# Attention blocks through DRAM: which side of the round trip is cut into four transfers

## The chip, the cores and the metric

The kernel runs on one core of a Trainium2 chip. The metric is the device time of one execution in microseconds (us). A core has five engines with a queue each: TensorE (PE in the profile, its weight loads PEld), VectorE (DVE), ScalarE (ACT), GpSimd (POOL) and SyncE (SP). SP computes nothing here; its queue issues nearly all DMA transfers, in program order, so a transfer that waits holds up every transfer behind it.

## The reference

A gated cross-attention block followed by a mixture of experts, all in float32. For each of 32 batch entries, 112 latent rows of 256 features attend to 375 context rows and to themselves, 487 keys in all, with 16 heads of 64 features. The result, times tanh of a gate, is added to `x`; then each token goes through its best two of eight experts.

```python
x = layer_norm(x, ln_m_g, ln_m_b)                  # context, 375 rows
lat = layer_norm(latents, ln_l_g, ln_l_b)          # 112 rows
q = lat @ Wq
k, v = jnp.split(jnp.concatenate([x, lat], axis=1) @ Wkv, 2, axis=-1)
dots = jnp.einsum('bhid,bhjd->bhij', q, k) * scale
attn = jax.nn.softmax(dots, axis=-1)
out = jnp.einsum('bhij,bhjd->bhid', attn, v)       # then @ Wout
...
x = x + jnp.tanh(g_xattn[0]) * attention(x, ctx)
x = x + jnp.tanh(g_ffn[0]) * experts(layernorm(x)) # top 2 of 8, gelu
```

## The kernel before

The program is one long list of steps without hardware loops. The attention stage fills about the first 1490 us, the expert stage the rest; at the seam they overlap.

Attention goes by *units* `n` from 0 to 127. A unit is one batch entry with two pairs of heads, so four heads, and two units (two batch entries, the same heads) make a *period*; there are 64. Scores are computed with queries on the partitions: the 112 queries lie as four groups of 28, each padded to 32, and the 487 keys, padded to 512, on the free axis. The exponentials of a unit fill a buffer `ex` (`exs[n % 3]`) of 128 partitions by 2048 float32, that is 8 KB a partition and 1 MB in all. The second matmul, probabilities times values, needs keys on the partitions instead. The turn is made in two steps:

- `turn_blocks` (L574): VectorE transposes every 32x32 block of `ex` in place, inside its group of 32 partitions. Partition `a*32+j` then holds, for query group `a`, key `j` of each block of 32 keys; on the free axis lies the block number `k` (0 to 3, the slowest), then heads, chunks of 128 keys and the query.
- a round trip through DRAM that exchanges `a` and `k`: `send_blocks` (L580) writes the unit to a DRAM buffer `turned[n % 4]`, and `take_blocks` (L587) reads it back as `exT`, where partition `k*32+j` is a key within a chunk of 128 and the free axis holds `a` first. `exT` has two buffers, one for each unit of a period.

The sends and the returns are issued on SP's queue, among the loads of inputs (`xin` L274, `cin` L278, `x` L626) and the transfers with which expert weights are read, added up by POOL and written back as `ws` (`piece_in` L1375 and L1379, `piece_out` L1415 and L1419).

The order of work is written out by hand. A period begins with `attend` of the period before (L600, 64 matmuls that read both `exT` buffers); then come the scores (L536) and exponentials (L555) of the next period's two units, and ten slots (two groups of five) with the steps of the table `PLAN`: `norm` (L569), `turn_blocks`, the query, key and value projections, and the sends `s0` and `s1`. The returns of a period are issued after its second slot:

```python
if h == 1 and not late and n < LAST - 2:
    for s in (n, n + 1):
        take_blocks(s)
if h == 1:
    do(after)                     # loads and pieces
if h == 1 and n == LAST - 2:      # in the last period: after them
    for s in (n, n + 1):
        take_blocks(s)
```

So a period's two units are sent in the period before, come back early in the period itself, and are read by `attend` at the beginning of the next one. A return can't start before `attend` has finished with the old contents of its buffer, nor before the unit's sends have landed. Waits are set by the framework from the tiles that an instruction reads and writes. Transfers from SP and ACT take eight completion semaphores in turn; a transfer also waits until the one that used its semaphore before, eight transfers earlier, has landed.

Of the kernel before, what the change touches and what calls it, by code (L numbers as in the profile page):

```python
# [23 lines left out]
def kernel(  # L24
# [20 lines left out]
    nc = tc.nc  # L45
# [38 lines left out]
    KTB, EXB, ETB = 4, 3, 2  # L84
# [18 lines left out]
    QB, QW, Q = 4, 32, S // 4  # L103
# [17 lines left out]
    turned = [dram.tile([QB, QW, QB, 2 * NCK * 2 * QW], F32, name=f"turned_{n}") for n in range(4)]  # L121
# [70 lines left out]
    if True:  # L192
# [309 lines left out]
        pss, nmx, sm, exT = {}, {}, {}, {}  # L502
# [3 lines left out]
        exs = [const.tile([P, QB, 2, NCK, 2, QW], F32, name=f"ex_{n}") for n in range(EXB)]  # L506
# [68 lines left out]

        def send_blocks(n, eng=nc.sync):


            for a in range(QB):
                eng.dma_start(  # L580
                    turned[n % 4][:, :, a, :].rearrange("k j n -> j k n"),
                    exs[n % EXB][a * QW : (a + 1) * QW].rearrange("j k q c h r -> j k (q c h r)"),
                )

        def take_blocks(n):
            exT[n] = soft.tile([P, QB, 2, NCK, 2, QW], F32, tag="exT", name=f"exT_{n}", bufs=ETB)
            nc.sync.dma_start(  # L587
                exT[n].rearrange("p a q c h r -> p (a q c h r)"),
                turned[n % 4].rearrange("k j a n -> (k j) (a n)"),
            )  # L590

        def attend(j):

# [930 lines left out]
        norm(1, 0)  # L1524
        turn_blocks(0, 1)
        send_blocks(0)
        units[0, 1][6]()
        norm(1, 1)
        turn_blocks(1, 0)
        weight_sums(0, 2)  # L1530
        units[0, 1][1]()
        turn_blocks(1, 1)
        send_blocks(1)
        units[1, 0] = seven(1, 0, 0)
        for kv, k in PROLOGUE:
# [17 lines left out]
        for n in range(LAST):  # L1553
# [17 lines left out]
            def step(what, period=period, beside=beside, qn=qn):  # L1571
                s, p = int(what[1]), int(what[-1])
                if what[0] == "q":
                    for j in qn:
                        q_unit(j // NG, j % NG + NG * s)
                elif what[0] in "kv":
                    at = beside[what[0]]
                    if at[1] < (UNITS, UNITS // 2)[at[0]]:
                        if at not in units:
                            units[at] = seven(*at)  # L1580
                        units[at][p - 1]()
                elif period + 1 < UNITS:
                    s += 2 * (period + 1)
                    if what[0] == "n":
                        norm(s, p)
                    elif what[0] == "t":
                        turn_blocks(s, p)
                    else:
                        send_blocks(s)
# [24 lines left out]
            k = n - 44  # L1614
# [89 lines left out]
            for h in range(5):  # L1704
                for what in PLAN[5 * late + h].split():
                    step(what)
                do(pe[h])
# [4 lines that stand above are left out]
                    do(after)  # L1712
                if h == 1 and n == LAST - 2:
                    for s in (n, n + 1):
                        take_blocks(s)
                if h == 4:
                    break
                then_ = soon_[:]
                del soon_[:]
                do(then_)  # L1720
                for part in dve[h]:
                    part()

                if outgoing and (h % 2 == 0 or n > LAST - NG):
                    outgoing.pop(0)()
                if extra and not (late and h > 1 and isinstance(extra[0], tuple)):
                    do(extra.pop(0))
# [3 lines left out]
        r, _ = route_parts(g, nc.vector)  # L1731
# [130 lines left out]
```

## Time and profile before

| what | us |
|---|---|
| median of three runs (lowest, highest) | 1905.92 (1905.05, 1910.44) |
| the profiled execution, its own time | 1907.72 |
| its span in the profile | 1905.9 |
| PE busy | 1876.3 |
| DVE busy | 1353.5 |
| ACT busy | 1136.4 |
| POOL busy | 992.5 |

The DMA queue that SP and ACT feed, q1, moved 413.31 MB in 247232 packets, and its packets took 73.6% of the 16 DMA engines' span. The 512 sends are of 256 KB each and the 128 returns of 1024 KB. The median issue of a send takes SP 691 ns and that of a return 412 ns.

An engine's busy time says how much it did, not whether it set the end: that is read from the waits, in which each engine's idle time is put down to what ended it. The `L` numbers are lines of the kernel before. The profile was taken on one execution, so sums made from its rows stand against that execution's own time.

### The profile page before, as it was taken

What the parts mean: (1) busy time and instruction counts of PE and PEld (TensorE: products, weight loads), DVE (VectorE), ACT (ScalarE), POOL (GpSimd) and SP (SyncE); (2) the same over time, 40 slices, a digit from 0 to 9 for tenths busy, and PEclk for the clock granted to TensorE, in tenths of its full rate; (3) what the DMA queues carried; (4) which work ended last, traced back from release to release, by engine and by line L of the source; (5) the groups of instructions that cost most, each with busy time, mean ns of one, the idle gap of its engine ahead of it and who ended that gap; (6) DMA issues with size and microseconds to landing.
All of it is one profiled execution on the core that took longest, in us unless ns stands there. A gap on an engine that the chain in (4) does not pass through costs nothing. (4 is left out here: it accounts for less than half of the span.)

```text
span 1905.9 us, 38258 instructions
## 1 busy us (share of the span) xinstructions
PE 1876.3 (98%) x12560; PEld 1433.5 (75%) x12560; DVE 1353.5 (71%) x2868; ACT 1136.4 (60%) x2718; POOL 992.5 (52%) x1475
## 2 busy tenths in 40 slices
PE   8999999999999999999999999999999999999998
PEld 4667777677777676777676777677677999999887
DVE  6787878787877878787878787878776477844111
ACT  5767666666776666667766666666756334434333
POOL 6433333435445746585556655753334588877212
PEclk9999999999999999999999999999999999999999
DMA  7777766767788888798979898896668786897872
GB/s 202 193 229 209 214 196 198 205 182 205 226 227 265 253 246 251 230 280 250 271 224 284 233 268 242 252 265 195 198 184 256 244 240 180 245 336 232 231 205 46
DMA packets 261049, 433.23 MB, mean 227 GB/s; under 512 B 30728, under 2 KB 149072, under 8 KB 244464
## 3 DMA queue, kind: packets, MB, share of 16 engines
q1 hardware_dynamic: 247232, 413.31, 73.6%
q0 software_dynamic: 11328, 15.33, 4.2%
q10 hardware_dynamic: 2288, 2.12, 0.4%
q8 instruction: 101, 1.65, 0.3%
q14 instruction: 100, 0.82, 0.1%
HBM read 301.37 MB, written 172.28 MB: 249 GB/s over the span
## 5 line engine op out<-in xcount | busy, mean ns | idle before, releaser
L555 ACT ACTIVATE ex<-bank,nmx 128x512 f32<-128x512 f32 x512 | 343.6, 697 | 85.7 <-DVE nmx L546 85.2
L569 ACT ACTIVATE ex<-ex,rc 128x512 f32<-128x512 f32 x512 | 342.7, 721 | 76.1 <-DVE rc L566 75.4
L546 DVE TENSOR_REDUCE nmx<-bank 128x1 f32<-128x487 f32 x512 | 298.6, 655 | 85.9 <-PE bank L536 83.6
L574 DVE STREAM_TRANSPOSE ex<-ex 128x1024 f32<-128x1024 f32 x256 | 314.9, 1230 | 19.5 <-ACT ex L569 15.7
L487 POOL TENSOR_TENSOR vv<-tmpv,vv 128x512 f32<-128x512 f32 x64 | 82.1, 1282 | 404.1 <-ACT vv L475 403.4
L536 PE MATMUL bank<-kT,qTs 64*128 64x487 f32 x1024 | 236.3, 588 | 3.0 <-DVE kvT L365 1.7
L600 PEld LDWEIGHTS bank<-exT,vv 128*64 128x64 f32 (+1 forms) x4096 | 198.9, 137 | 30.9 <-issue 22.6
L600 PE MATMUL bank<-exT,vv 128*64 128x112 f32 (+1 forms) x4096 | 213.0, 261 | 2.3 <-DMA exT<-turned 1.6
L617 ACT COPY outT<-bank 128x256 f32<-128x256 f32 (+3 forms) x160 | 40.0, 314 | 263.9 <-PE bank L600 258.8
L434 PE MATMUL bank<-tT,wkv_s 128*128 128x487 f32 x378 | 186.3, 575 | 0.5 <-ACT ex L555 0.5
L439 PE MATMUL bank<-wkv_s,tT 128*128 128x256 f32 x768 | 186.7, 379 | 0.0
L439 PEld LDWEIGHTS bank<-wkv_s,tT 128*128 128x128 f32 x768 | 144.8, 190 | 43.3 <-issue 21.4
L1164 POOL DMA_INDIRECT out_dram<-y,xs x60 | 93.5, 1558 | 154.0 <-DVE y L1191 77.9
L536 PEld LDWEIGHTS bank<-kT,qTs 64*128 64x128 f32 x1024 | 98.8, 187 | 99.2 <-issue 69.9
L1405 POOL TENSOR_TENSOR piece<-piece 128x128 f32<-128x128 f32 x256 | 116.9, 457 | 89.7 <-DMA piece<-in_L_ffn_w_dram 78.3
L439 PE MATMUL bank<-wkv,kvT 128*128 128x256 f32 x512 | 132.0, 380 | 0.8 <-ACT ex L555 0.6
L439 PEld LDWEIGHTS bank<-wkv,kvT 128*128 128x128 f32 x512 | 94.6, 190 | 50.5 <-issue 33.9
L484 DVE TENSOR_TENSOR kT<-bank,kT 128x487 f32<-128x487 f32 x189 | 120.8, 640 | 14.0 <-POOL kT L487 7.5
L434 PE MATMUL bank<-kvT,wkv 128*128 128x487 f32 x252 | 130.1, 598 | 0.0
L484 DVE TENSOR_TENSOR vv<-bank,vv 128x512 f32<-128x512 f32 x192 | 128.2, 668 | 1.8 <-POOL vv L487 0.2
L1219 ACT ACTIVATE h<-h,b 128x256 f32<-128x256 f32 x160 | 66.1, 495 | 91.9 <-DVE h L1230 53.2
L373 PEld LDWEIGHTS bank<-kvT,wq_sb 128*128 128x128 f32 x512 | 96.2, 188 | 28.9 <-issue 17.0
(296 smaller groups left out, 3718.2 us busy)
## 6 DMA issues: line engine op xcount, KB each, us to landing
turned<-ex SPq DMA_DIRECT2D x512, 256.0 KB
exT<-turned SPq DMA_DIRECT2D x128, 1024.0 KB
w<-in_L_ffn_w_dram SPq DMA_DIRECT2D x132, 256.0 KB
w_s<-ws SPq DMA_DIRECT2D x80, 256.0 KB
w_t<-ws SPq DMA_DIRECT2D x80, 256.0 KB
w_b2x<-in_L_ffn_w_dram SPq DMA_DIRECT2D x38, 512.0 KB
ws<-piece SPq DMA_DIRECT2D x64, 256.0 KB
cin<-in_ctx_dram SPq DMA_DIRECT2D x32, 336.0 KB
```

The lines of the kernel that those rows point to most:

```text
L373: nc.tensor.matmul(ps, lhsT=wq_sb[:, k, i * P : (i + 1) * P], rhs=kvT[g][:, k, :, SC:NK], start=(k == 0), stop=(k == KD - 1),)
L434: nc.tensor.matmul(ps, lhsT=w[:, 0, i * P : (i + 1) * P], rhs=x[:, :NK], start=True, stop=True)
L439: nc.tensor.matmul(ps[:, c, :], lhsT=x[:, (2 * h + c) * P : (2 * h + c + 1) * P], rhs=w[:, 1, i * P : (i + 2) * P], start=True, stop=True,)
L484: nc.vector.tensor_tensor(v[o], ps, v[r], ALU.add)
L536: nc.tensor.matmul(ps[:, :NK], lhsT=qT[b // 2, i][r, b % 2].rearrange("p a i -> p (a i)"), rhs=kT[b, i][r, :], start=True, stop=True,)
L546: nc.vector.tensor_reduce(nmx[b, i][:, j : j + 1], pss[b, i][j][:, :NK], AX.X, ALU.max, negate=True)
L555: nc.scalar.activation(exs[n % EXB][:, :, p, :, j, :], ps[j].rearrange("p (c k r) -> p k c r", c=NCK, r=QW), AF.Exp, bias=nmx[b, i][:, j : ...
L569: nc.scalar.mul(t, t, rc[:, j : j + 1])
L574: nc.vector.transpose(t, t)
L600: nc.tensor.matmul(ps[y * DH : (y + 1) * DH, r, x * S : (x + 1) * S].rearrange("p (a i) -> p a i", a=QB), lhsT=vv[j // 2, c // 2][:m, c % ...
L1164: add = nc.gpsimd.indirect_dma_start(out=outf, out_offset=bass.IndirectOffsetOnAxis(ap=xs[t][:, b, D + 1 : D + 2].bitcast(I32), axis=0), i ...
L1405: nc.gpsimd.tensor_tensor(o, l, r, op) for o, l, r, op in ops
```

## The change

The same 1 MB of each unit goes out and comes back with the same bytes in the same places of DRAM. Before, the exchange of `a` and `k` is made on the way out: four sends, one for each query group, each from 32 partitions in runs of 2 KB, scattered into `turned`; the return is one transfer into 128 partitions with runs of 8 KB. After, the send is one transfer from 128 partitions in 8 KB runs, and the exchange is made on the way back: four returns, one for each `k`, each into 32 partitions with runs of 2 KB. The places of the sends and returns in the program's order are the same. The number of transfers per unit stays five.

```diff
         def send_blocks(n, eng=nc.sync):
 
-
-            for a in range(QB):
-                eng.dma_start(
-                    turned[n % 4][:, :, a, :].rearrange("k j n -> j k n"),
-                    exs[n % EXB][a * QW : (a + 1) * QW].rearrange("j k q c h r -> j k (q c h r)"),
-                )
+            eng.dma_start(
+                turned[n % 4].rearrange("a j k n -> (a j) (k n)"),
+                exs[n % EXB].rearrange("p k q c h r -> p (k q c h r)"),
+            )
 
         def take_blocks(n):
             exT[n] = soft.tile([P, QB, 2, NCK, 2, QW], F32, tag="exT", name=f"exT_{n}", bufs=ETB)
-            nc.sync.dma_start(
-                exT[n].rearrange("p a q c h r -> p (a q c h r)"),
-                turned[n % 4].rearrange("k j a n -> (k j) (a n)"),
-            )
+            for k in range(QB):
+                nc.sync.dma_start(
+                    exT[n][k * QW : (k + 1) * QW].rearrange("p a q c h r -> p a (q c h r)"),
+                    turned[n % 4][:, :, k, :].rearrange("a j n -> j a n"),
+                )
```

## The prediction

> **What bounds the kernel now.** I read part 1 of the page first, then the list of who waits for whom on TensorE (PE) and on SP's queue, then SP's timeline through one dense stretch, the DMA view of stretches that hold one kind of transfer, and last the packet records.
>
> ```profile
> PE 1876.3 (98%) x12560; PEld 1433.5 (75%) x12560; DVE 1353.5 (71%) x2868; ACT 1136.4 (60%) x2718; POOL 992.5 (52%) x1475
> ```
>
> And from the waits of PE (who is waited for: us in total, times, longest):
>
> ```profile
> PE bank L600 <- DMA exT<-turned: 1.6, 1, 1.6
> ```
>
> PE sets the time. It is idle for 1905.9 - 1876.3 = 29.6 us, so no transfer change can win more than that; the idle time sits in the start-up, the expert stage and the drain. The wait above is all that PE waits for returned blocks today: one, in the last attend. So the change acts only by making PE late, or by removing that 1.6 us.
>
> ```profile
> 606.00:1260.00 654.00, 653.93 (x4179) 465.53 (x4179) 515.39 (x1072) 439.13 (x1042) 391.02 (x651) 1.00 0.87 254
> 629.00:650.00 21.00, 21.00 (x142) 14.54 (x142) 16.55 (x31) 14.17 (x34) 18.29 (x23) 1.00 0.96 296
> ```
>
> These are stretches of the span: length, PE, PEld, DVE, ACT, POOL busy, clock, DMA share, GB/s. PE has no gap, but the DMA engines are 87% busy over 654 us and 96% in some periods. The cover is thin there.
>
> ```profile
> 627.61 1.45 SPq L1419 DMA_DIRECT2D ws<-piece  x1
> 629.61 4.23 SPq L580 DMA_DIRECT2D turned<-ex  x4
> 633.94 1.18 SPq L274 DMA_DIRECT2D xin<-in_x_dram  x1
> 635.16 1.59 SPq L278 DMA_DIRECT2D cin<-in_ctx_dram  x2
> 636.79 0.90 SPq L1375 DMA_DIRECT2D piece<-in_L_ffn_w_dram  x2
> 637.89 0.38 SPq L1419 DMA_DIRECT2D ws<-piece  x1
> 638.37 0.92 SPq L587 DMA_DIRECT2D exT<-turned  x2
> ```
>
> This is SP's queue between a pair's second send (629.61) and its returns (638.37). Only the returns have 8 KB packets on this queue (16384 = 128 x 128), so the last of each 128 tells when it ends; PE resumed 0.74 us after it in the one place where it waited (1489.20 to 1489.94). For this pair that is 648.29 + 0.74 = 649.03, and the attend that reads it begins at 649.61: 0.58 us of slack. I did this for all 63 pairs before the last. The twelve smallest slacks are 0.58, 0.65, 0.76, 1.39, 1.56, 1.67, 1.73, 1.91, 2.08, 2.12, 2.26, 2.30 us; 21 lie under 4.5; the median is near 6.7. All the small ones but one lie between 578 and 1282 us.
>
> **Price of the two shapes.** Three windows of the DMA view: only sends (258.5 to 262 us), only 2 KB loads into all 128 partitions (1478 to 1482), almost only returns (1482.5 to 1487).
>
> ```profile
> DMA packets 418, 0.77 MB, mean 221 GB/s; under 512 B 41, under 2 KB 41, under 8 KB 418
> ...
> DMA packets 742, 1.36 MB, mean 341 GB/s; under 512 B 77, under 2 KB 77, under 8 KB 742
> ...
> DMA packets 262, 1.86 MB, mean 414 GB/s; under 512 B 23, under 2 KB 23, under 8 KB 40
> ```
>
> The engines are 98 to 100% busy in all three. So 1.05 MB costs 1.05 / 0.221 = 4.7 us as four quarters of 32 partitions, 3.1 us as 2 KB runs over all partitions, 2.5 us as 8 KB runs.
>
> **Sends, removed and added.** 512 sends become 128. Data: the one 8 KB send to DRAM has no row; the return is its mirror, so 2.5 us, 2.2 saved on each of two sends a period. It can't cost more than the 4.7 us of today's send, which moves the same bytes in more pieces; that end would hand back nothing. Issue on SP: 4.23 us for four in the lines above becomes one of about 0.41 (median of a whole-block return), 3.8 saved. Little of that reaches the returns: xin (L274) waits there for PE for 1.1 us whatever the sends do, so the returns can be issued perhaps 0.7 us earlier.
>
> **Returns, removed and added.** 128 become 512. Data: their shape is the send's mirror (32 partitions, 2 KB runs), so I take 4.7 us each: +2.2 each, +4.4 a pair. The low end is the 341 GB/s row, 3.1 us, +1.2 a pair. The high end is the stretch of a send in which its first two quarters are alone, about 190 GB/s in the DMA view of 258.9 to 260.9 us: 5.5 us, +6 a pair. I choose 4.7 because the partition count, not the run length, separates the first two rows.
> [...]
> Issue on SP: eight issues at the send's median 0.69 us are 5.5 us instead of 0.95. Behind them stand two piece loads (0.9) and the next first send, issued 7.6 us after the returns here (645.93). 5.5 + 0.9 = 6.4 fits; at the crowded 4.23 / 4 = 1.06 each it is 9.4 and that send is 1.8 us late, whose waiters are its own returns some 12 us later. Left at nothing; the high end carries it.
>
> **Semaphores.** Transfers use eight completion semaphores in turn, so a transfer waits for the one eight before it. Eight returns take them all; the piece load behind waits for the first quarter (1.2 us of data, issued 5 us before) and passes. PE's first matmul on each buffer waits for four transfers instead of one: 384 more waits. A wait record on PE's queue is 51 ns, so between 0 and 384 x 51 ns = 20 us; I take 0, because PE's queue runs ahead (one such record at 146.53 us precedes its matmul at 150.05) and the existing ones leave PE no gap. StreamTranspose (L574) and exp (L555) wait for one send instead of four: about 0.1 us earlier a block, at nothing.
>
> **The sum.** In a dense period a pair's returns end 4.4 us later for their own data, 2.2 earlier because the second send leaves the ring sooner; what the first send saves is idle ring before the second, which is held by DVE, and the 0.7 us of earlier issue I set against ring gaps. Shift: +2.2 us. PE loses what exceeds each slack: (2.2 - 0.58) + (2.2 - 0.65) + (2.2 - 0.76) + 0.81 + 0.64 + 0.53 + 0.47 + 0.29 + 0.12 + 0.08 = 7.6 us over ten periods. The cover is the slack itself: at a shift of 1 the loss is 1.0 us, at 3 it is 17.5, at 4.5 it is 45. The low end (1.2 - 2.2, below zero) loses nothing. The last pair has no cover:
>
> ```profile
> 1487.36 0.99 PE L600 MATMUL bank<-exT,vv 128*64 128x112 f32 x16 [0.72 <-DVE h L1237]
> 1489.94 3.94 PE L600 MATMUL bank<-exT,vv 128*64 128x112 f32 x48 [1.59 <-DMA exT<-turned]
> ```
>
> PE already waits there for the second return. Its data comes up to 4.4 us later, no send is left to hand anything back; the first return's delay meets PE's own 0.72 us wait. Between 1.2 and 4.4, I take 3.0. Sum: 7.6 + 3.0 = 10.6 us. The profiled execution took 1907.72 us for a span of 1905.9, and its like would take 1918.3; that is 1.8 above the median of 1905.92, so the median becomes 1916.5.
>
> **Rivals.**
> 1. *The cover holds* (not slower). Place: the returns between 578 and 1282 us. If the ring gives back what it takes (a 2 KB return at 341 GB/s, or the sends' 2.2 us each both counting), the shift is 1 us or less, and only the tail costs: 1.0 + 1.2 to 3 = 2 to 4 us, 1908 to 1910. It decides from a shift below about 1.5 us (2.6 us lost). For it: PE has shown no wait at all so far. Against: three slacks under 0.8.
> 2. *The DMA engines become the bound.* At 5.5 us a return the pair costs 6 us more and the sends give 4.4 back, so 1.6 us more work a period. At 96% of 21 us (20.2 us) this makes 21.8: over. Backlog then carries from period to period; with a shift of 4.5 to 6 the losses are 45 to 85 us, less what PE's lateness itself frees, so 20 to 50: 1926 to 1956. For it: the 0.96 row. Against: the mean of 0.87.
> 3. *Faster.* The one wait (1.6 us) and the start-up hold nearly all that transfers could free; more than 3 us has no place to come from.
> 4. *Nothing changes in the transfers* is excluded by the diff: the pieces on both sides are fixed by the patterns.
>
> **How the numbers follow.** Forecast (1911.7 to 1926) 0.45; cover holds 0.27; DMA-bound 0.24; faster 0.04. About 0.3% (5.7 us) is what a measurement of this kernel can tell from no change, so faster 0.04, same 0.27, slower 0.69. The range takes in the cover's case from 1904 and the DMA-bound case up to 1942, leaving out its upper half and the faster case. The forecast's own range is 1911 to 1926.
>
> **What would show it.** Right: a window with only sends near 400 GB/s, one with only returns near 220; PE waits on exT at L600 in some ten periods between 578 and 1282 us, a few us in sum each at most; the last attend's wait 3 to 6 us instead of 1.6. Wrong: returns at 340 GB/s or more; no new L600 wait; or DMA share at 1.0 over hundreds of us with waits growing from period to period; or PE gaps at L600 with the returns long landed, which would be the 384 waits.

## The result, and the profile after

Five runs of the changed kernel took 1920.75 to 1925.73 us, median 1922.93; the kernel before, now with five runs (the three of the table among them), 1905.05 to 1913.14, median 1910.44. The ratio is 1.0073 (95% interval 1.005 to 1.0097): slower by some 14 us. The prediction was a median of 1916.5, that is 10.6 us more than the 1905.92 it was built on, in a range of 1904 to 1942.

The profiled execution took 1920.97 us for a span of 1919.3, against 1907.72 and 1905.9: 13.4 us more of span. In the changed kernel the send is L578, the return L586 and the attend L599. PE's busy time grew by 4 us and its idle time by 9. Part 1 of its page:

```profile
PE 1880.5 (98%) x12560; PEld 1438.5 (75%) x12560; DVE 1352.7 (70%) x2868; ACT 1136.5 (59%) x2718; POOL 992.3 (52%) x1475
```

The waits of PE in the changed kernel (us in total, times, longest). They were one wait of 1.6 us on returned blocks:

```profile
PE bank L599 <- DMA exT<-turned: 6.5, 4, 3.1
PE bank L599 <- issue: 3.6, 1, 3.6
```

The 3.6 us put down to "issue" are the first wait of the last attend. The trace's record of it on PE's queue runs from 1490.50 to 1494.45 us and waits for the semaphores of the first unit's first and fourth quarter; the fourth one's last count came at 1494.41. So this is a wait for a return too. SP's timeline of the changed kernel in the same dense period as shown before:

```profile
628.77 0.33 SPq L578 DMA_DIRECT2D turned<-ex  x1
629.19 0.38 SPq L274 DMA_DIRECT2D xin<-in_x_dram  x1
629.63 2.02 SPq L278 DMA_DIRECT2D cin<-in_ctx_dram  x2
631.75 0.97 SPq L1374 DMA_DIRECT2D piece<-in_L_ffn_w_dram  x2
637.07 0.38 SPq L1418 DMA_DIRECT2D ws<-piece  x1
637.50 4.28 SPq L586 DMA_DIRECT2D exT<-turned  x8
641.83 1.54 SPq L1374 DMA_DIRECT2D piece<-in_L_ffn_w_dram  x2
```

The second send costs SP 0.33 us instead of 4.23, and eight returns 4.28 instead of 0.92. The loads behind the send go out 4 us earlier, but `ws` (L1418) then waits for POOL until 637.07, and the returns gain nothing in this period: they start 0.9 us sooner on the profile's clock, but the second send is 0.8 us earlier there too. The DMA view of two stretches of the changed kernel, the first with sends alone (809 to 811 us), the second with returns alone (245 to 252):

```profile
DMA packets 103, 0.84 MB, mean 422 GB/s; under 512 B 0, under 2 KB 0, under 8 KB 0
...
DMA packets 799, 1.46 MB, mean 209 GB/s; under 512 B 84, under 2 KB 84, under 8 KB 799
```

The two rates have changed sides: before, sends ran at 221 GB/s and returns at 414. What it does to PE, first in a period of the dense stretch, then at the last attend:

```profile
832.80 0.99 PE L599 MATMUL bank<-exT,vv 128*64 128x112 f32 x16
835.68 3.69 PE L599 MATMUL bank<-exT,vv 128*64 128x112 f32 x38 [1.89 <-DMA exT<-turned]
...
1494.61 1.76 PE L599 MATMUL bank<-exT,vv 128*64 128x112 f32 x16 [3.60 <-issue]
1499.46 4.75 PE L599 MATMUL bank<-exT,vv 128*64 128x112 f32 x48 [3.09 <-DMA exT<-turned]
```

PE runs its first 16 matmuls, which read the first unit, and then stops for the second. After these two stops the same matmuls take longer: 48 of them 4.18 and 4.75 us, against 2.53 at 650.64 us, behind a stop of 0.87 us. The windows of the changed kernel show the granted clock there (length, PE, PEld, DVE, ACT, POOL busy, clock, DMA share, GB/s):

```profile
830.00:840.00 10.00, 8.11 (x76) 6.50 (x76) 5.13 (x11) 1.55 (x4) 7.28 (x10) 0.83 1.08 326
1490.00:1505.00 15.00, 8.31 (x76) 7.41 (x75) 1.96 (x4) 3.74 (x10) 1.77 (x5) 0.66 1.07 283
606.00:1260.00 654.00, 650.45 (x4155) 463.87 (x4155) 510.57 (x1062) 435.68 (x1036) 385.87 (x643) 1.00 0.93 251
```

The granted clock falls to half for 3.41 us at 836 us and for 10.24 us from 1495. The kernel before had one such stretch of 3.41 us at its last attend, and one at 66 us, which this execution lacks. Its window over the last attend:

```profile
1485.00:1500.00 15.00, 12.69 (x108) 11.40 (x108) 3.90 (x11) 3.90 (x10) 2.58 (x7) 0.89 0.97 333
```

By the starts of the attends in the two profiles the 13.4 us divide so:

| stretch | us | made of |
|---|---|---|
| to 628 us | -0.8 | start-up +0.9; the half-clock stretch at 66 us is missing, -1.7 |
| 628 to 1428 us | +5.9 | three waits at L599 (0.87, 1.89, 0.69) = 3.45; half clock 3.41 / 2 = 1.7; 0.7 not put down to anything |
| to the start of the last attend | +2.2 | its first wait 3.60 against 0.72; other waits -0.7 |
| from there to the end | +6.1 | its second wait 3.09 against 1.59; half clock 1.9 more; the expert stage +2.7 |

The 1.9 us are read from the lengths: the first 16 matmuls of the last attend take 1.76 us against 0.99, the other 48 take 4.75 against 3.94, and the stretch runs 0.7 us, at half rate, past them. Half of 10.24 - 3.41 would be too much, since PE stands still for 3.09 us of the stretch and a lower clock costs nothing there. The +2.7 can't be put down to the change: what follows the last attend takes 412.1 us before and 415.1 after, but 413.7 to 417.3 us in the eight kernels below.

### The profile page after: what moved, and what is told of

It reads as the page before. It is cut to its first block, busy times and chain, and to the rows that moved or that the text cites. A ratio compares the mean times of both kernels' runs of the same rounds, so it can differ in the third digit from the quotient of the medians.

```text
span 1919.3 us, 38314 instructions
## 1 busy us (share of the span) xinstructions
PE 1880.5 (98%) x12560; PEld 1438.5 (75%) x12560; DVE 1352.7 (70%) x2868; ACT 1136.5 (59%) x2718; POOL 992.3 (52%) x1475
## 3 DMA queue, kind: packets, MB, share of 16 engines
q8 instruction: 102, 1.67, 0.4%
## 5 line engine op out<-in xcount | busy, mean ns | idle before, releaser
L599 PEld LDWEIGHTS bank<-exT,vv 128*64 128x64 f32 (+1 forms) x4096 | 202.0, 139 | 39.3 <-issue 28.8
L599 PE MATMUL bank<-exT,vv 128*64 128x112 f32 (+1 forms) x4096 | 216.8, 264 | 10.1 <-DMA exT<-turned 6.5
```

The lines of the kernel that those rows point to most:

```text
L599: nc.tensor.matmul(ps[y * DH : (y + 1) * DH, r, x * S : (x + 1) * S].rearrange("p (a i) -> p a i", a=QB), lhsT=vv[j // 2, c // 2][:m, c % ...
```

## The experiments

Theory M: a quarter of 32 partitions moves at half the rate (209 GB/s against 414), so returns land later, and PE waits where the slack is short and at the last pair. Theory W: the 384 further waits on PE's queue, or the greater number of transfers, cost the time. Rival R: the 2 KB runs on the return do. Each ratio is to runs of the kernel before on the same chip.

**The last pair in the old shape, all others in the new** (and next, the reverse).

```diff
+            if n >= B * NG - 2:
+                ...  # four sends, one return
+            else:
+                ...  # one send, four returns
```

> The changed kernel, but the last two units (the last period's pair) go out in four sends and come back in one return, as before the change. Theory M (late returns: a return cut into quarters of 32 partitions moves at about 220 GB/s, so a pair lands some 2 us later; PE stalls in the few periods with little slack, and most of all at the last pair): the changed kernel's profile shows 3.60 + 3.09 us of PE waits at the last attend against 0.72 + 1.59 before, and 10.2 us of half clock right behind them against 3.4. So this kernel should win back (6.69 - 2.31) + 6.8 / 2 = 7.8 us of the 13 and stand 4 to 7 us over the kernel before (ratio 1.002 to 1.004), with its last attend waiting 1 to 2.5 us and the waits between 640 and 1110 us still there. Theory W (the 384 further semaphore waits on PE's queue cost the time): 126 of 128 units still have them, so it stays at 1.007.

Measured: ratio 1.0029 (1.0017 to 1.0042). Its PE waits on returned blocks, and a window over its last attend:

```profile
PE bank L612 <- DMA exT<-turned: 3.5, 4, 1.1
...
1486.00:1501.00 15.00, 13.90 (x137) 12.78 (x136) 6.55 (x15) 3.89 (x10) 3.38 (x13) 1.00 1.03 373
```

Three of the four waits are those of the dense stretch (0.91, 1.00 and 0.54 us, at 651, 836 and 1107), the fourth is the last attend's. There is no half clock in that window; the one stretch of it, 3.41 us from 1478.8, lies ahead of it, behind a stop of PE for `xs`, which is no part of the round trip. The expectation's 7.8 us counted half clock also while PE stood still; with 1.9 us for it, 6.3 were to be won back. More than half the loss, 0.44 of 0.73%, went with two units of 128.

> The kernel before, but the last two units go out in one send and come back in four returns. Theory M: the last attend waits 5 to 7 us in all instead of 2.3, and the clock falls for longer behind it: 5 to 9 us over the kernel before (ratio 1.003 to 1.005), and no PE wait on returned blocks anywhere else. Theory W: six waits more in all, nothing measurable: ratio 1.000. If the middle of the attention stage carries the loss instead, also 1.000.

Measured: ratio 1.0023 (1.001 to 1.0035), a little under the range expected. Its PE waits on returned blocks, PE in its last attend, and the window there:

```profile
PE bank L612 <- DMA exT<-turned: 4.0, 1, 4.0
PE bank L612 <- issue: 2.9, 1, 2.9
...
1490.07 1.45 PE L612 MATMUL bank<-exT,vv 128*64 128x112 f32 x16 [2.89 <-issue]
1495.55 4.75 PE L612 MATMUL bank<-exT,vv 128*64 128x112 f32 x48 [4.03 <-DMA exT<-turned]
...
1486.00:1501.00 15.00, 8.07 (x78) 7.22 (x77) 1.29 (x2) 2.74 (x8) 1.77 (x5) 0.66 1.06 265
```

Waits of 6.9 us in the last attend and none earlier; half clock for 10.24 us again. Together the two halves make 0.29 + 0.23 = 0.52%, within the interval of the whole change. This speaks against W: the six further returns of one pair cost about as much as the 378 of all the others together.

**The return cut in four, but over all partitions.**

```diff
-            nc.sync.dma_start(exT[n] ..., turned[n % 4].rearrange("k j a n -> (k j) (a n)"))
+            for a in range(QB):
+                nc.sync.dma_start(exT[n][:, a] ..., turned[n % 4][:, :, a, :].rearrange("k j n -> (k j) n"))
```

> The kernel before with its four sends, and the return cut into four as well, but by query group: each of the four brings 2 KB runs into all 128 partitions. It has the four-fold returns, the 2 KB runs, the eight semaphores taken by a pair and the 384 further waits on PE of the changed kernel, and none of its quarters of 32 partitions. Theory M: a return moves at 340 GB/s or more, as the 2 KB weight loads do, so a pair lands 1.1 us later or less than before: 0 to 3 us over the kernel before (ratio 0.999 to 1.002), DMA share a little higher. Theory W, or run length as the price: as slow as the changed kernel, 1.007, or slower since the sends give nothing back.

Measured: ratio 1.0015 (1.0004 to 1.0026). Returns alone (244 to 250 us), and the dense stretch:

```profile
DMA packets 861, 1.58 MB, mean 264 GB/s; under 512 B 89, under 2 KB 89, under 8 KB 861
...
606.00:1260.00 654.00, 653.92 (x4180) 465.60 (x4179) 515.62 (x1072) 439.40 (x1042) 391.23 (x650) 1.00 0.90 254
```

It has as many wait records on PE's queue as the changed kernel (660, of which 256 at the attends; before 463 and 39), and PE loses nothing in the dense stretch. So neither the waits nor the four transfers cost what was seen, and W is out. The rate was over-rated: 264 GB/s, not the 340 of the weight loads, though the engines were only 88% busy in that window. Whether the 2 KB runs or the eight issues hold it down, this run doesn't separate. Of its loss of some 2.9 us the last attend shows 0.9 (it waits 3.2 us instead of 2.3); the rest is not located.

**The quarters in another order.**

```diff
-            for k in range(QB):
+            for k in (0, 2, 1, 3):
```

> The changed kernel with the four returns of a unit in the order 0, 2, 1, 3 instead of 0, 1, 2, 3. Same sizes, runs, waits and number of transfers. In a send of the kernel before the first two quarters ran at 190 GB/s and the stretch in which the second and third met at about 290. [...] If only the number of partitions in one transfer counts, the rate stays at 220 and the ratio at 1.007. Theory W: 1.007.

Measured: ratio 1.0042 (1.0026 to 1.0057); returns alone (244 to 252 us):

```profile
DMA packets 1005, 1.83 MB, mean 229 GB/s; under 512 B 112, under 2 KB 112, under 8 KB 1005
```

The rate rises with the order alone, to 229 GB/s; the changed kernel has 209 in the window shown and 216 in this one. An estimate from the 290 GB/s at which a send's second and third quarter met was 250 to 290, too high. In the dense stretch the waits fall from 3.45 to 1.4 us; the last attend still waits 6.6 us, with 6.83 us of half clock behind it. The interval of this ratio overlaps that of the change, so the gain over the changed kernel is likely, not settled.

**Quarters on both ways**, in 8 KB runs on the return, and then two halves of 64 partitions instead of four quarters. The low and high halves differ from the even and odd ones only in which partitions go together.

```diff
+            for k in range(QB):                             # quarters
+                nc.sync.dma_start(exT[n][k * QW : (k + 1) * QW] ..., turned[n % 4][k] ...)
...
+            for s in (slice(0, 64), slice(64, 128)):        # low and high half
+            for s in (slice(0, 128, 2), slice(1, 128, 2)):  # even and odd half
+                nc.sync.dma_start(exT[n][s] ..., turned[n % 4].rearrange("k j a n -> (k j) (a n)")[s])
```

> The kernel before with its four sends, and the return cut into four quarters of 32 partitions in 8 KB runs. The slow side is now on both ways. If the quarter's price is its 32 partitions, a pair's returns take about 9.5 us of data instead of 5.2 although the runs are 8 KB, and the sends give nothing back: the pair lands some 4 us later, and by the table of slacks PE loses 35 to 45 us in some 20 periods; the transfers also fill the ring in the dense stretch (0.96 of 21 us plus 4.4 us), so it may be more. With the last attend's wait: 35 to 70 us over the kernel before, ratio 1.018 to 1.037. If instead 2 KB runs are the price, quarters of 8 KB runs return at 400 GB/s and the ratio is 1.000 to 1.002.

> The kernel before with its four sends, and the return in two transfers of 8 KB runs: partitions 0 to 63, then 64 to 127. If the price grows with the smallness of the partition count, 64 partitions run at some 300 GB/s: a pair lands 2 us later, 5 to 10 us over before, ratio 1.003 to 1.006. [...] If only the number of transfers or waits counted: 1.000 to 1.001.

> As the run with a low and a high half, but the two transfers take the even and the odd partitions, 64 each. Same bytes, runs, transfers and waits. [...] If the number of partitions in a transfer decides, as slow as the low and high halves.

Measured: quarters 1.0116 (1.0101 to 1.0131), low and high halves 1.0143 (1.0126 to 1.016), even and odd halves 1.0006 (0.9997 to 1.0016). Returns alone, in that order (246 to 254, 244 to 252 and 248 to 252 us):

```profile
DMA packets 333, 1.84 MB, mean 229 GB/s; under 512 B 109, under 2 KB 109, under 8 KB 109
...
DMA packets 271, 1.83 MB, mean 228 GB/s; under 512 B 48, under 2 KB 48, under 8 KB 48
...
DMA packets 223, 1.47 MB, mean 367 GB/s; under 512 B 44, under 2 KB 44, under 8 KB 44
```

This settles what sets the rate. A low half, 64 partitions in 8 KB runs, is as slow as a quarter of 32; every second partition, also 64, comes back at 367 GB/s, and the kernel is back at the time of before. The packet records of all periods agree. From its first packet to its last a pair takes, in the median, 7.6 us whole (the kernel before) and 7.3 in even and odd halves, but 10.6 in low and high halves, 10.4 in quarters of 8 KB runs and 11.0 in quarters of 2 KB runs (the changed kernel). So it isn't the number of partitions, and the length of the runs has only a small part (R), but which partitions a transfer touches. Nor is it the place in DRAM: the changed kernel's quarters read 2 KB runs from all over the 1 MB, a low half reads one piece of 512 KB, and both are slow (209 and 228 GB/s). Why neighbouring partitions are slower together than alternate ones, 228 against 367 GB/s, no trace here shows.

The loss with quarters on both ways, 22 us, is below the 35 to 70 expected: eight waits of 0.7 to 2.0 us in the attention stage before the last attend, 10.7 us in all, where the table of slacks gave 35 to 45. Both errors of that table, told in the next section, act here too.

**Neither side cut.**

```diff
+            nc.sync.dma_start(turned[n % 4].rearrange("a j k n -> (a j) (k n)"), exs[n % EXB] ...)
...
+            nc.sync.dma_start(exT[n] ..., turned[n % 4].rearrange("k j a n -> (k j) (a n)"))
```

> One send and one return per unit, both whole, in 8 KB runs; the exchange of query group and key block is left out, so the second matmul gets the blocks in another order (same shapes and number of instructions). What the round trip costs today in all: the ring loses 4.4 us of work a period. Theory M says that the kernel before was covered but for the last attend's 1.6 us (and 0.7 us of PE's own), so this gains 0 to 4 us: ratio 0.998 to 1.000. If slow transfers also cost PE something that no wait shows (slower weight loads, a slower VectorE), it gains more than 5 us.

Measured: ratio 0.9994 (0.9985 to 1.0003). This kernel leaves out the exchange of `a` and `k`, so it is no version to use; it prices the round trip. In the kernel before the slow side costs nothing that could be measured, at most 0.15% (2.9 us) by the interval, and none of these kernels beats it clear of the noise.

## Why the prediction was right, and where its steps were off

- *The shapes' price* was right: 422 GB/s for the whole send and 209 for the quartered return, against 414 and 221 put in. The reason given (the partition count) was wrong: the halves, 228 GB/s low and high and 367 even and odd, show that it is which partitions go together.
- *The shift of a pair's landing*, 2.2 us, was too large. From the packet records of 62 pairs, from first packet to landing a pair takes 11.65 us instead of 8.31 (medians), +3.3, and begins 1.7 us sooner after the attend before it, where 0.7 was allowed. The landing is 1.6 us later in the median. In the twelve tightest pairs the mean is 1.2, spread from 0.6 earlier to 3.2 later.
- *The slack was measured to the wrong matmul.* I took the attend's first one. The second unit's return, which lands last, is needed only by the 17th, 0.8 us later in the median; the lines at 832.80 and 835.68 us show PE running 16 matmuls and then stopping. With both errors the dense stretch lost 3.45 us in three periods, not 7.6 in ten.
- *The half clock was left out.* One stop of PE in the dense stretch had 3.41 us of half clock behind it and those of the last attend 10.24: 1.7 us in the dense stretch and 1.9 more than before at the last attend. No term of the sum held it, though the kernel before showed one at that same place.
- *The last pair*, 3.0 us, was mis-sized: its waits grew from 2.3 to 6.7 us, +4.4, the upper end that I had given; with the clock it is 6.3. Of the 4.4, 2.9 stand at the first return, whose delay I let vanish in PE's own wait of 0.72 us. So 10.6 came near the 12.5 us between the medians in part by luck, since the stages' errors offset each other: 7.6 against 5.2 in the middle, 3.0 against 6.3 at the end.
- *Semaphores at nothing* held. The trace shows the eight completion semaphores, with 185 of the 1480 transfers each. The return cut by query group has the same waits and no loss in the dense stretch. The 384 waits were also too many: there are 197 more wait records, since one record can wait for two semaphores, as the one at 1490.50 us does. SP's eight issues took 4.28 us, 0.53 each. Transfers behind the returns do wait for a quarter's semaphore now (SP's waits show 43.8 us of it ahead of sends, 54 times), but within time that they would have waited for VectorE: all 128 sends are issued 0.03 us after their second transpose ends.
- *Rivals.* The cover held in all but three periods, which is most of the first rival; what it left out was the last pair's true price. The DMA engines came to 93% over the dense stretch, from 87, and did not become the bound: PE was idle there for 3.6 of 654 us. (By the slacks a shift of 6 us costs 80 us, not the 85 of that rival.)

## What to carry to other kernels

Where a transposing round trip must be cut on one side, cut the side whose landing has the longer cover; and price a transfer by the partitions that it touches together, not by its size alone: 64 partitions came back at 228 or at 367 GB/s here. Look at the last iteration by itself: a transfer hidden 126 times is bare in the last two, and here these two made a third of the loss by one run (0.23 of 0.73%) and three fifths by the other (0.44). Measure a transfer's slack to the first instruction that reads its last bytes, and price a stop of PE with the half-clock stretch that may follow, 3.41 us behind 1.89 here.

## What the runs showed of the hardware that was not expected

A stop of PE of 1.89 us was followed by a stretch of half clock longer than itself: PE went on at 835.68 us, and the clock was 0.5 from 835.85 us for 3.41 us. The length of a stop does not decide it alone. Of two stops at 65 us that differ by 0.01 us, the 1.67 us of the kernel before were followed by 3.41 us of half clock and the 1.66 us of the changed kernel by none (granted clock 0.89 and 1.00 from 60 to 75 us). With the return cut by query group the last attend stopped for 1.48 and 1.68 us, and its 48 matmuls took 2.53 us, as at 650.64 us in the changed kernel, where the granted clock was 1.00. What does decide it was not shown.

Transfers of every second partition, two for a unit, returned at 367 GB/s, near the 414 of the whole; cutting a tile this way costs almost nothing (ratio 1.0006) where a low and a high half cost 1.4%, some 27 us.
